# Graph layer and expert layer: node sums for two tiles at a time, gate logits by expert for four tiles at a time

## The chip, the core and the metric

The kernel runs on one core of one Trainium2 chip. A core has five engines with queues of their own: TensorE (PE, matrix products; its weight loads are shown apart as PEld), VectorE (DVE), ScalarE (ACT), GpSimd (POOL) and SyncE (SP), and 16 DMA engines that move data for all of them. PE writes into PSUM, from which DVE or ACT copy into SBUF. The metric is the time of one execution on the device in microseconds (us), as a median over several; every engine works through its own queue in order, and waits at semaphores for others.

## The reference, cut to what matters

There are N = 12500 nodes with D = 256 features, 212500 weighted edges sorted by destination (17 to a node on average), and E = 8 experts.

```
xn  = layernorm(x)
agg = segment_sum(xn[src] * edge_weight, dst)      # (N, 256)
x1  = x + agg @ W.T + b
t   = layernorm(x1)
logits = t @ gate_w + gate_b                       # (N, 8)
e   = argmax(softmax(logits));  p = its probability
# the first C = 1954 tokens of each expert are kept, in token order
y   = relu(t @ w1[e] + b1[e]) @ w2[e] + b2[e]      # hidden size 1024
out = x1 + nan_to_num(y * p * kept)
```

## The kernel before

A tile is 128 rows. Nodes make 98 tiles (the last has 84 rows), edges 1661 tiles.

**Start.** `table()` normalises x into the DRAM table `feat`, while the first 112 edge tiles are gathered from x itself.

**Main loop.** Each turn of the `while` loop near the end (L822) writes, in this order, one `gather` (L582, an indirect DMA on POOL's queue that fetches 128 source rows into a buffer `m`, of which there are 32), then at most one scatter from `pool_q` (or a step of a finished page's ending), some selection matrices `h` (`onehot`, L590), one `product` (L599: h.T @ m, added in PSUM over a group of 15 edge tiles; 16 turns behind its gather), one step of `nodes()` and one step of `experts()`. The generators' `yield`s set which turn an instruction is written in, and that order is kept on each engine's queue (the schedule is manual). Each group's sum is copied to an SBUF tile `ws` (L602) and stands in `sums`.

**Nodes.** Node rows and groups of edges don't line up. For a tile t, `groups_of(t)` gives the two or three groups that can hold its edges; `shift` (L608) makes for each a 128 x 128 matrix `s` of 0 and 1 (L612) that moves group rows to node rows, and L635 adds `sums[g].T @ s` for the two halves of the features. ACT copies the result (`aT`, L639), L644 multiplies by the weights, and DVE adds x and the bias into `rt` (L647, L648) and takes the statistics (L180, L181). A tile waits for its last group (`while gs[-1] not in sums`).

**Routing.** Tiles are taken in 14 chunks: eleven of eight tiles, then five, four and one. At a chunk's end `route` (L246) takes the root of the variance on ACT (L185) and inverts it on DVE, stores `rt` to `out`, and for each tile normalises (L214), transposes twice on PE (L271), copies to SBUF (`xT`, L274), multiplies with `gw_sb` (L279: the tokens are the weights, eight columns move through) and adds the bias (L281). Then come argmax (L296 to L306), prefix sums over tokens (L314, L315), the exponential (L317), the place of each token in the pages of its expert (L338), and `put`, a scatter per tile on POOL (L341). `listing` finds pages that are full; `last` lists the part-filled ones.

**Experts.** `experts` takes the pages in order. A page holds 128 tokens of one expert (some are taken as pairs). SP loads the page (`pg`, L439) and 2 MB of weights (L446 to L452), DVE normalises it (`xg`, L459), PE transposes it (L468), multiplies (L483, L494), and `finish` does the rest up to a scatter into `out` (`send`, L525, on POOL). A page starts at the earliest twenty turns after its load; steps of a single page are 2.3 turns apart. All PSUM tiles of nodes and routing come from one pool of two buffers (`psum`, L242); transposes of routing and of pages share one buffer (`pT`).

After the loop stand branches (`rest`, and a second way of summing) that the inputs here don't enter.

Of the kernel before, what the change touches and what calls it, by code (L numbers as in the profile page):

```python
# [94 lines left out]
def gnn_moe_kernel(ctx: ExitStack, tc: tile.TileContext, x, src, dst, ew, wT, gb, gate_w, gate_b,  # L95
# [13 lines left out]
    cols = consts.tile([P, P], F32, name="cols")  # L109
    nc.gpsimd.iota(cols, pattern=[[1, P]], base=0, channel_multiplier=0,  # L110
                   allow_small_or_imprecise_dtypes=True)
    pcol = consts.tile([P, 1], F32, name="pcol")
# [42 lines left out]
    gateb_sb = consts.tile([P, E], F32, name="gateb_sb")  # L155
# [63 lines left out]
    class Ffn:  # L219
# [26 lines left out]
        def route(self, rt, ln, t0, nt, rows):  # L246
# [9 lines left out]
            def normal(j):  # L256
                xn[j] = p3.tile([P, D], F32, name="xn1", bufs=3)
                ln_apply(xn[j][:rows, :], rt[:rows, j, :D], ln, r, j, rows)
# [7 lines left out]
            for j in range(nt):  # L266
                if j + 2 < nt:
                    normal(j + 2)
                pt = self.ps_t.tile([P, 512], F32, name="pT")
                for k in range(2):  # L270
                    nc.tensor.transpose(pt[:, k * P:k * P + rows], xn[j][:rows, k * P:(k + 1) * P],  # L271
                                        ident[:rows, :rows])
                xT = p3.tile([P, 2, P], F32, name="xT", bufs=3)
                nc.scalar.copy(xT[:, :, :rows],  # L274
                               pt[:, :2 * P].rearrange("p (k r) -> p k r", k=2)[:, :, :rows])
                yield
                pl = self.psum("pl")[:, :E]
                for k in range(2):
                    nc.tensor.matmul(pl[:rows, :], xT[:, k, :rows], gw_sb[:, k, :],  # L279
                                     start=(k == 0), stop=(k == 1))  # L280
                nc.vector.tensor_add(lgs[:rows, j, :], pl[:rows, :], gateb_sb[:rows, :])  # L281
# [277 lines left out]
    with tc.tile_pool(name="edges", bufs=1) as edges:  # L559
# [8 lines left out]
        with tc.tile_pool(name="p2", bufs=32) as p2, tc.tile_pool(name="p2h", bufs=12) as p2h, \  # L568
# [36 lines left out]
            def nodes():  # L605
                xs, shifts = [], {}

                def shift(t):  # L608

                    for g in groups_of(t) if t < NT else ():  # L610
                        s = p2o.tile([P, P], F32, name="s", bufs=8)
                        nc.vector.tensor_scalar(s, cols, float(P * t), win[:, g:g + 1], op0=ALU.add,  # L612
                                                op1=ALU.is_equal)
                        shifts[t, g] = s

                for c, (t0, nt, rows) in enumerate(CHUNKS):
                    rt = p3.tile([P, CH, RW], F32, name="rt")
                    ln = ln_new(p3)
                    for t in range(t0, t0 + nt):
# [5 lines left out]
                        if t == 0:  # L625
                            shift(t)
# [363 lines left out]
```

## Time and profile before

| | |
|---|---|
| median of three runs | 2569.41 us (2568.65 to 2575.24) |
| the profiled execution | 2575.36 us, its span 2573.6 us |
| mean granted clock of TensorE | 0.867 |
| POOL: gathers from `feat` (L582) | 1549, 972 ns each |
| PE: products of edges (L599) | 3322 passes, 451 ns each |
| PE: sums of nodes (L635) | 1116 passes, 299 ns each |
| PE: gate logits (L279) | 392 passes, 272 ns each |
| DVE: selection matrices s (L612) | 279, 308 ns each |

A line of a group gives the source line, the engine, the operation, the tiles (out<-in), shapes and count, then the busy time and the mean of one, then the engine's idle time just before and what ended it. In the order of time, a row has the start, the length, the engine, the line and the tiles; "x6" means six instructions in a row, and brackets give the idle time before and who ended it. Matmuls overlap in the records, so their pitch (the time between starts) is shorter than their listed length; an f32 matmul shows as two passes. A turn is one pass of the main loop.

### The profile page before, as it was taken

How to read it: one execution, taken by the hardware profiler on the slowest of the kernel's cores; microseconds unless marked ns; L12 is line 12 of the kernel's file. 1: busy time of each engine (PE TensorE's matmuls, PEld its weight loads, DVE VectorE, ACT ScalarE, POOL GpSimd, SP SyncE). 2: the span in 40 equal slices, each digit the busy share in tenths (PEclk: the TensorE clock that was granted, in tenths of full speed). 3: DMA queues.
4: the chain of work that ended last, by engine and by line, in shares of the span. 5: the costliest groups of instructions: out<-in, count | busy, mean ns of one | idle time of the engine just before them, and what ended most of it. 6: DMA issues, size and time to landing. Idle time of an engine off the chain costs nothing. (4 is left out here: it accounts for less than half of the span.)

```text
span 2573.6 us, 30236 instructions
## 1 busy us (share of the span) xinstructions
PE 2046.4 (80%) x9082; PEld 1599.7 (62%) x9082; DVE 1177.0 (46%) x4287; ACT 504.9 (20%) x1315; POOL 1805.4 (70%) x1859
## 2 busy tenths in 40 slices
PE   2467788797799698698699699698698797698797
PEld 1345545575577477477487487477476574487686
DVE  6775433444344344354453444444443443454432
ACT  5750000111012012012012012012011110122232
POOL 7647777777777777777777777777777777777111
PEclk9678666799799799799799799799799797799898
DMA  8759434644654654654654654654654354497485
GB/s 282 252 172 368 127 109 124 193 145 122 211 166 123 219 157 122 209 165 121 204 170 122 201 175 122 204 170 123 194 177 121 110 186 122 138 309 247 153 273 176
DMA packets 264700, 455.60 MB, mean 177 GB/s; under 512 B 44799, under 2 KB 190406, under 8 KB 264520
## 3 DMA queue, kind: packets, MB, share of 16 engines
q0 software_dynamic: 88800, 240.41, 30.5%
q1 hardware_dynamic: 136210, 174.68, 21.1%
q10 hardware_dynamic: 39510, 38.41, 4.6%
q8 instruction: 77, 1.26, 0.2%
q14 instruction: 103, 0.84, 0.1%
HBM read 387.86 MB, written 67.83 MB: 177 GB/s over the span
## 5 line engine op out<-in xcount | busy, mean ns | idle before, releaser
L582 POOL DMA_INDIRECT m<-feat,src_i x1549 | 1506.2, 972 | 493.0 <-issue 222.1
L599 PE MATMUL pw<-m,h 128*128 128x256 f32 x3322 | 1114.9, 451 | 408.7 <-DMA m<-feat,src_i 297.8
L599 PEld LDWEIGHTS pw<-m,h 128*128 128x128 f32 x3322 | 654.0, 219 | 701.9 <-DMA m<-feat,src_i 406.2
L590 DVE TENSOR_SCALAR h<-cols,rel,w_sb 128x128 f32<-128x128 f32 x1549 | 467.0, 360 | 405.6 <-PE pw L599 397.3
L483 PE MATMUL ph<-gT,w_sb 128*128 128x256 f32 (+1 forms) x1856 | 362.7, 346 | 0.0
L494 PE MATMUL py<-w_sb,hT 128*128 128x256 f32 x1456 | 349.8, 385 | 0.0
L483 PEld LDWEIGHTS ph<-gT,w_sb 128*128 128x128 f32 x1856 | 308.7, 199 | 33.3
L494 PEld LDWEIGHTS py<-w_sb,hT 128*128 128x128 f32 x1456 | 274.6, 193 | 35.1
L487 ACT ACTIVATE hT<-ph,b_sb 128x256 f32<-128x256 f32 (+1 forms) x464 | 167.9, 426 | 419.4 <-PE ph L483 409.7
L525 POOL DMA_INDIRECT out<-z,tok x91 | 91.1, 1001 | 153.2 <-DVE tok L522 111.7
L635 PEld LDWEIGHTS ms<-s,ws 128*128 128x128 f32 x1116 | 177.1, 216 | 18.2 <-issue 3.7
L635 PE MATMUL ms<-s,ws 128*128 128x128 f32 x1116 | 176.3, 299 | 3.4 <-DVE s L612 3.3
L647 DVE TENSOR_TENSOR rt<-xt,ms 128x256 f32<-128x256 f32 x98 | 41.2, 420 | 287.8 <-PE ms L644 287.7
L602 ACT COPY ws<-pw 128x256 f32<-128x256 f32 x111 | 41.4, 373 | 631.6 <-PE pw L599 631.6
L582 POOL DMA_INDIRECT m<-in_x,src_i x112 | 108.1, 965 | 53.6 <-issue 20.1
L504 DVE TENSOR_TENSOR y<-py,b_sb 128x512 f32<-128x512 f32 (+1 forms) x58 | 33.4, 576 | 240.4 <-PE py L494 240.4
L341 POOL DMA_INDIRECT buf<-rt,to x98 | 98.9, 1009 | 54.0 <-issue 19.2
L459 DVE TENSOR_SCALAR xg<-pg 128x256 f32<-128x256 f32 x91 | 35.3, 418 | 174.1 <-DMA pg<-buf 174.1
L507 ACT ACTIVATE y<-y,pg 128x256 f32<-128x256 f32 x91 | 42.6, 502 | 340.4 <-DVE y L504 294.5
L644 PE MATMUL ms<-wT_sb,aT 128*128 128x256 f32 x392 | 107.4, 399 | 2.4 <-ACT aT L639 2.4
L639 ACT COPY aT<-ms 128x256 f32<-128x256 f32 x98 | 36.5, 373 | 275.6 <-PE ms L635 269.9
L644 PEld LDWEIGHTS ms<-wT_sb,aT 128*128 128x128 f32 x392 | 77.4, 199 | 15.8 <-ACT aT L639 4.4
(159 smaller groups left out, 1253.6 us busy)
## 6 DMA issues: line engine op xcount, KB each, us to landing
w_sb<-in_w SPq DMA_DIRECT2D x116, 1024.0 KB, 11.4
m<-feat,src_i POOLq DMA_INDIRECT x1549, 2.8
buf<-fill SPq DMA_DIRECT2D x13, 1300.0 KB, 18.4
xt<-in_x ACTq DMA_DIRECT2D x97, 128.0 KB, 2.4
xt<-in_x SPq DMA_DIRECT2D x12, 1024.0 KB, 8.1
feat<-xn ACTq DMA_DIRECT2D x12, 1024.0 KB, 9.7
out<-rt ACTq DMA_DIRECT2D x11, 1024.0 KB, 4.9
pg<-buf SPq DMA_DIRECT2D x33, 260.0 KB, 13.4
```

What stands on the lines that cost most here:

```text
L341: s = nc.gpsimd.indirect_dma_start(out=buf[:, :], out_offset=bass.IndirectOffsetOnAxis(ap=to[:, j, :], axis=0), in_=rt[:rows, j, :], in_of ...
L483: nc.tensor.matmul(ph[:, c:c + n], w1_sb[:, k, f * P:(f + 1) * P], xT[:, k * n:(k + 1) * n], start=(k == 0), stop=(k == 1))
L487: nc.scalar.activation(hT[:, f, :n], ph[:, c:c + n], AF.Relu, bias=b1_sb[:, f:f + 1])
L494: nc.tensor.matmul(py[:, a, :], hT[:, f, a * P:(a + 1) * P], w2_sb[:, f, :], start=(f == 0), stop=(f == F // P - 1))
L507: nc.scalar.activation(y[:, a, :], y[:, a, :], AF.Copy, scale=pg[:, a, D + 2:D + 3])
L525: s = nc.gpsimd.indirect_dma_start(out=out[:, :], out_offset=bass.IndirectOffsetOnAxis(ap=to[:, a, :], axis=0), in_=z[:, a, :], in_offset= ...
L582: nc.gpsimd.indirect_dma_start(out=m, out_offset=None, in_=x[:, :] if k < RAW else feat[:, :], in_offset=bass.IndirectOffsetOnAxis(ap=src_ ...
L590: nc.vector.tensor_scalar(h, cols, rel[:, k:k + 1], w_sb[:, k:k + 1] if w is None else w, op0=ALU.is_equal, op1=ALU.mult)
L599: nc.tensor.matmul(product.pw, hs.pop(k), ms.pop(k), start=(j == 0), stop=last)
L602: nc.scalar.copy(ws, product.pw)
L635: nc.tensor.matmul(pa[:, k * P:(k + 1) * P], sums[g][:, k * P:(k + 1) * P], shifts[t, g], start=(g == gs[0]), stop=(g == gs[-1]))
L644: nc.tensor.matmul(px[:rows, :], aT[:, k * P:k * P + rows], wT_sb[:, k, :], start=(k == 0), stop=(k == 1))
```

## The change

The selection matrices become 256 columns wide: `turns` lists pairs of tiles within a chunk (a single one where a chunk is odd), `groups` the union of their groups, and `shift` makes one wide matrix for each group of the turn, with six buffers instead of eight. The sums are made for both tiles at once (256 columns move through PE for each group and half of the features), one ACT copy takes them (512 columns, one buffer instead of two), and the projection follows tile by tile, with a step of its own for each. The loads of x keep two tiles ahead of a pair, with five buffers.

In `route`, transposes of two tiles fill one PSUM tile and one copy takes them to `xT`, which now holds four tiles in one buffer. Then `gw_sb` is the weights (eight columns) and up to 512 tokens move through; the logits come out with experts on partitions. ACT adds the bias from `gateb_sb`, now one value per partition, into `lT`; PE transposes each tile's part back (eight columns each), and one DVE copy fills `lgs` for four tiles.

```diff
@@ -106,9 +106,10 @@
     make_identity(nc, ident)
     ones = consts.tile([P, P], F32, name="ones")
     nc.vector.memset(ones, 1.0)
-    cols = consts.tile([P, P], F32, name="cols")
-    nc.gpsimd.iota(cols, pattern=[[1, P]], base=0, channel_multiplier=0,
+    cols2 = consts.tile([P, 2 * P], F32, name="cols")
+    nc.gpsimd.iota(cols2, pattern=[[1, 2 * P]], base=0, channel_multiplier=0,
                    allow_small_or_imprecise_dtypes=True)
+    cols = cols2[:, :P]
     pcol = consts.tile([P, 1], F32, name="pcol")
     nc.gpsimd.iota(pcol, pattern=[[1, 1]], base=0, channel_multiplier=1,
                    allow_small_or_imprecise_dtypes=True)
@@ -152,7 +153,7 @@
     gb_sb = consts.tile([P, D], F32, name="gb_sb")
     wT_sb = consts.tile([P, 2, D], F32, name="wT_sb")
     gw_sb = consts.tile([P, 2, E], F32, name="gw_sb")
-    gateb_sb = consts.tile([P, E], F32, name="gateb_sb")
+    gateb_sb = consts.tile([E, 1], F32, name="gateb_sb")
 
     keep = ctx.enter_context(tc.tile_pool(name="keep", bufs=1))
     run = keep.tile([P, E], F32, name="run")
@@ -254,7 +255,7 @@
             xn = {}
 
             def normal(j):
-                xn[j] = p3.tile([P, D], F32, name="xn1", bufs=3)
+                xn[j] = p3.tile([P, D], F32, name="xn1", bufs=4)
                 ln_apply(xn[j][:rows, :], rt[:rows, j, :D], ln, r, j, rows)
 
             for j in range(min(nt, 2)):
@@ -263,22 +264,38 @@
             nc.vector.tensor_copy(rt[:rows, :nt, D:D + 1], ln[1][:rows, :nt, 0:1])
             nc.vector.tensor_copy(rt[:rows, :nt, D + 1:D + 2], r[:rows, :nt, None])
             yield
-            for j in range(nt):
-                if j + 2 < nt:
-                    normal(j + 2)
-                pt = self.ps_t.tile([P, 512], F32, name="pT")
+
+            for j0 in range(0, nt, 4):
+                n4 = min(4, nt - j0)
+                xT = p3.tile([P, 2, 4 * P], F32, name="xT", bufs=1)
+                for j1 in range(j0, j0 + n4, 2):
+                    n2 = min(2, nt - j1)
+                    pt = self.ps_t.tile([P, 512], F32, name="pT")
+                    for j in range(j1, j1 + n2):
+                        if j + 2 < nt:
+                            normal(j + 2)
+                        for k in range(2):
+                            c = (k * n2 + j - j1) * P
+                            nc.tensor.transpose(pt[:, c:c + rows], xn[j][:rows, k * P:(k + 1) * P],
+                                                ident[:rows, :rows])
+                    c = (j1 - j0) * P
+                    n = (n2 - 1) * P + rows
+                    nc.scalar.copy(xT[:, :, c:c + n], pt[:, :2 * n2 * P].rearrange(
+                        "p (k r) -> p k r", k=2)[:, :, :n])
+                    yield
+                    yield
+                n = (n4 - 1) * P + rows
+                pl = self.psum("pl")
                 for k in range(2):
-                    nc.tensor.transpose(pt[:, k * P:k * P + rows], xn[j][:rows, k * P:(k + 1) * P],
-                                        ident[:rows, :rows])
-                xT = p3.tile([P, 2, P], F32, name="xT", bufs=3)
-                nc.scalar.copy(xT[:, :, :rows],
-                               pt[:, :2 * P].rearrange("p (k r) -> p k r", k=2)[:, :, :rows])
+                    nc.tensor.matmul(pl[:E, :n], gw_sb[:, k, :], xT[:, k, :n], start=(k == 0),
+                                     stop=(k == 1))
+                lT = p3.tile([E, 4 * P], F32, name="lT", bufs=1)
+                nc.scalar.activation(lT[:, :n], pl[:E, :n], AF.Identity, bias=gateb_sb)
                 yield
-                pl = self.psum("pl")[:, :E]
-                for k in range(2):
-                    nc.tensor.matmul(pl[:rows, :], xT[:, k, :rows], gw_sb[:, k, :],
-                                     start=(k == 0), stop=(k == 1))
-                nc.vector.tensor_add(lgs[:rows, j, :], pl[:rows, :], gateb_sb[:rows, :])
+                pb = self.psum("pb")[:, :4 * E].rearrange("p (j e) -> p j e", e=E)
+                for j in range(n4):
+                    nc.tensor.transpose(pb[:rows, j, :], lT[:, j * P:j * P + rows], ident[:E, :E])
+                nc.vector.tensor_copy(lgs[:rows, j0:j0 + n4, :], pb[:rows, :n4, :])
             yield
 
             def small(name, last=E, dt=F32):
@@ -605,48 +622,64 @@
             def nodes():
                 xs, shifts = [], {}
 
-                def shift(t):
-
-                    for g in groups_of(t) if t < NT else ():
-                        s = p2o.tile([P, P], F32, name="s", bufs=8)
-                        nc.vector.tensor_scalar(s, cols, float(P * t), win[:, g:g + 1], op0=ALU.add,
-                                                op1=ALU.is_equal)
-                        shifts[t, g] = s
-
+
+                turns = [(t, min(2, t0 + nt - t)) for t0, nt, _ in CHUNKS for t in range(t0, t0 + nt, 2)]
+
+                def groups(i):
+                    t, n = turns[i]
+                    return range(groups_of(t)[0], groups_of(t + n - 1)[-1] + 1)
+
+                def shift(i):
+
+                    for g in groups(i) if i < len(turns) else ():
+                        t, n = turns[i]
+                        s = p2o.tile([P, 2 * P], F32, name="s", bufs=6)
+                        nc.vector.tensor_scalar(s[:, :n * P], cols2[:, :n * P], float(P * t),
+                                                win[:, g:g + 1], op0=ALU.add, op1=ALU.is_equal)
+                        shifts[i, g] = s
+
+                turn = 0
                 for c, (t0, nt, rows) in enumerate(CHUNKS):
                     rt = p3.tile([P, CH, RW], F32, name="rt")
                     ln = ln_new(p3)
-                    for t in range(t0, t0 + nt):
-                        for i in range(len(xs), min(t + 3, NT)):
-                            x_ = p3.tile([P, D], F32, name="xt", bufs=4)
+                    while turn < len(turns) and turns[turn][0] < t0 + nt:
+                        t1, n = turns[turn]
+                        for i in range(len(xs), min(t1 + n + 2, NT)):
+                            x_ = p3.tile([P, D], F32, name="xt", bufs=5)
                             r = min(P, N - i * P)
                             nc.scalar.dma_start(x_[:r, :], x[i * P:i * P + r, :])
                             xs.append(x_)
-                        if t == 0:
-                            shift(t)
-                        gs = groups_of(t)
+                        if turn == 0:
+                            shift(0)
+                        gs = groups(turn)
                         while gs[-1] not in sums:
                             yield
                         yield
-                        pa = ffn.psum("pa")[:, :2 * P]
-                        aT = p2o.tile([P, 2 * P], F32, name="aT")
+                        pa = ffn.psum("pa")
+                        aT = p2o.tile([P, 2, 2 * P], F32, name="aT", bufs=1)
                         for k in range(2):
                             for g in gs:
-                                nc.tensor.matmul(pa[:, k * P:(k + 1) * P],
-                                                 sums[g][:, k * P:(k + 1) * P], shifts[t, g],
+                                nc.tensor.matmul(pa[:, k * n * P:(k + 1) * n * P],
+                                                 sums[g][:, k * P:(k + 1) * P],
+                                                 shifts[turn, g][:, :n * P],
                                                  start=(g == gs[0]), stop=(g == gs[-1]))
                             yield
-                        nc.scalar.copy(aT, pa)
-                        shift(t + 1)
+                        nc.scalar.copy(aT[:, :, :n * P],
+                                       pa[:, :2 * n * P].rearrange("p (k r) -> p k r", k=2))
+                        turn += 1
+                        shift(turn)
                         yield
-                        px = ffn.psum("px")[:, :D]
-                        for k in range(2):
-                            nc.tensor.matmul(px[:rows, :], aT[:, k * P:k * P + rows], wT_sb[:, k, :],
-                                             start=(k == 0), stop=(k == 1))
-                        x1 = rt[:rows, t - t0, :D]
-                        nc.vector.tensor_add(x1, xs[t][:rows, :], px[:rows, :])
-                        nc.vector.tensor_add(x1, x1, gb_sb[:rows, :])
-                        ln_stats(ln, x1, t - t0, rows)
+                        for t in range(t1, t1 + n):
+                            px = ffn.psum("px")[:, :D]
+                            a = (t - t1) * P
+                            for k in range(2):
+                                nc.tensor.matmul(px[:rows, :], aT[:, k, a:a + rows], wT_sb[:, k, :],
+                                                 start=(k == 0), stop=(k == 1))
+                            x1 = rt[:rows, t - t0, :D]
+                            nc.vector.tensor_add(x1, xs[t][:rows, :], px[:rows, :])
+                            nc.vector.tensor_add(x1, x1, gb_sb[:rows, :])
+                            ln_stats(ln, x1, t - t0, rows)
+                            yield
                     yield from ffn.route(rt, ln, t0, nt, rows)
                     pool_q.extend(ffn.put)
                     last = c == len(CHUNKS) - 1
@@ -810,7 +843,7 @@
                             product(k)
                 nc.sync.dma_start(gb_sb, gb.partition_broadcast(P))
                 nc.sync.dma_start(gw_sb, gate_w.rearrange("(k p) e -> p k e", p=P))
-                nc.sync.dma_start(gateb_sb, gate_b.partition_broadcast(P))
+                nc.sync.dma_start(gateb_sb, gate_b.rearrange("(e a) -> e a", a=1))
                 return n * RB
 
             done = table()
```

## The prediction

> **What bounds the kernel now.** I read the page's first two parts, then POOL in the order of time, then PE in the order of time from the last gather on, then PE and the clock by stretches.
>
> The busiest engine by share is PE (80%), POOL has 70%. The order of time says otherwise:
>
> ```profile
> PE 2046.4 (80%) x9082; PEld 1599.7 (62%) x9082; DVE 1177.0 (46%) x4287; ACT 504.9 (20%) x1315; POOL 1805.4 (70%) x1859
> ...
> POOL 7647777777777777777777777777777777777111
> ```
>
> ```profile
> 931.35 0.95 POOL L582 DMA_INDIRECT m<-feat,src_i  x1 [0.30 <-PE ph L483]
> 932.60 0.94 POOL L582 DMA_INDIRECT m<-feat,src_i  x1 [0.30 <-PE pw L599]
> ...
> 2378.56 0.95 POOL L582 DMA_INDIRECT m<-feat,src_i  x1 [0.30 <-issue]
> 2379.82 1.00 POOL L525 DMA_INDIRECT out<-z,tok  x1 [0.30 <-issue]
> 2388.39 1.00 POOL L525 DMA_INDIRECT out<-z,tok  x1 [7.57 <-DVE tok L522]
> ```
>
> Each gather of 128 rows takes 0.95 us and 0.30 us follows it; from 190 us to the last gather at 2378.56 no gap of POOL is longer than 0.31, whatever the releaser named. About 1710 indirect DMAs stand there, 1.28 us each: 2190 us. So three stages: a start to 182 us, a body at POOL's pace, and a tail of 181 us from the last gather to the last instruction at 2559.8 (14 us of ending follow in the span).
>
> In the body PE waits for gathers, 297.8 us in the list of waits. From a product's end to the issue of the gather that takes its buffer again I find at least 29 us, and from a chunk's destinations (L338) to its first scatter at least 7.6 us. PE work in the body is covered by these.
>
> The tail is PE's (its last matmul ends there), with idle time:
>
> ```profile
> 2384.50 0.59 PE L599 MATMUL pw<-m,h 128*128 128x256 f32 x2
> 2384.93 1.78 PE L635 MATMUL ms<-s,ws 128*128 128x128 f32 x12
> 2387.18 1.13 PE L644 MATMUL ms<-wT_sb,aT 128*128 128x256 f32 x4 [0.46 <-ACT aT L639]
> 2388.15 3.73 PE L483 MATMUL ph<-gT,w_sb 128*128 128x128 f32 x32
> 2394.76 0.41 PE L468 MATMUL pT<-ident,xg 128*128 128x128 f32 x2 [2.88 <-DVE xg L459]
> ...
> 2415.41 0.41 PE L468 MATMUL pT<-ident,xg 128*128 128x128 f32 x2 [3.34 <-DVE xg L459]
> ...
> 2434.18 0.41 PE L468 MATMUL pT<-ident,xg 128*128 128x128 f32 x2 [2.82 <-DVE rt L264]
> ...
> 2445.51 0.20 PE L424 MATMUL ms<-c,page_of 128*1 128x8 f32 x2 [6.05 <-DVE c L422]
> ...
> 2453.34 0.44 PE L468 MATMUL pT<-ident,xg 128*128 128x128 f32 x2 [0.99 <-DVE xg L459]
> ```
>
> ```profile
> 2392.40:2395.80 3.40, 1.03 (x6) 0.99 (x7) 2.36 (x11) 1.83 (x7) 0.00 (x0) 0.99 1.08 373
> 2395.80:2402.60 6.80, 6.34 (x20) 4.91 (x19) 0.49 (x2) 0.74 (x2) 0.00 (x0) 0.50 0.06 16
> ...
> 2457.10:2558.60 101.50, 96.40 (x649) 88.75 (x647) 38.67 (x124) 40.00 (x130) 12.66 (x13) 1.00 0.84 268
> ```
>
> (Columns: stretch, length, busy us of PE, PEld, DVE, ACT, POOL, granted clock, DMA share, GB/s.) After a stretch with little PE work the clock is 0.50 for the next. From 2457.1 on the clock is 1.00 and expert pages follow each other at 7.58 us. Between 2384.9 and 2457.1 the last nodes are routed: 72.2 us, for four pages (about 30 us) and some 11 us of node work.
>
> **The change part by part.** Pitches at full clock: a 128-column pass 0.111 us (six from 912.47 to 913.14), a 256-column pass 0.216 (eight L494 in 1.73). An f32 matmul is two passes.
>
> *Work on PE.* Sums: 1116 passes of 128 columns, 124 us, become 764 of 256 and 20 of 128 (196 pairings of group and turn, not 279; two halves, two passes): 167 us, +43. Logits: 392 passes at 0.09 (four in 0.36), 35 us; after, 24 groups x 4 passes of 512 columns at 0.43, 41 us, and 98 small transposes at about 0.11, 11 us: +17. Together +60 us of PE, nearly all in the body, under the waits for gathers: 0. Without that cover it would be +60.
>
> *DVE and ACT.* Selection tiles: 279 x 0.236 = 66 us become 196 wide ones at 0.29 to 0.41 (L513 and L459, 256 columns), 57 to 80. Logit evictions: 98 x 0.166 become 26 x 0.2, -11. ACT: 196 copies x 0.372 = 73 become 100 x 0.5 and 26 logit evictions of 0.5, -10. In the body these are slack: 0. What they can still do is slow POOL. The Trainium skill ("GPSIMD Engine Reference", Specifications) has GpSimd's SBUF interfaces shared with VectorE, contended by its two-port modes; this speaks against wider one-source instructions, and the added 14 us at most, charged in full, would be +14. The row: the gather at 932.60 ran beside three selection tiles (932.19 to 932.86) in 0.94, the fastest there is. I take 0, range -2 to +4.
>
> *Order.* The written order of the changed kernel has every later step of a chunk, and every expert page, exactly four turns of the main loop later relative to the gathers; the scatters' and sends' order on POOL is the same, but one send moves behind the last gather: -1.3 us. Loads on SP move with their pages and stay behind the same scatters. The x loads on ACT's queue are issued in pairs, one more buffer deep: 0.
>
> *The tail*, walked along PE's new order. (a) Last product. Before it ends 6.4 us after its gather's issue, since PE still had 17 us of work in its last 14 turns (17.9 us of POOL). The new order has there 14 products (6.0) and one page (7.2), 13.2 us, so PE waits for the gather; a product can end 3.5 us after it. I take -2.2, with the send 2384.9 becomes 2381.4. (b) To the first page's transposes: the half page moved behind (0.2 + 1.7 + 1.7), the pair's sums (16 passes, 3.5 against 1.3; four groups against three), two projections (1.7 against 0.9), first layer 3.5: 12.3 us. DVE is late: after the first projection (at 8.2) two tiles of 1.6 each, the page's ending 2.0, variance, root 0.2 or with its table 1.5, inverse 1.0, two normalised tiles 0.7: 15.7 to 17.0. Queued behind it: the transposes of the first pair, ACT's copy, then the page's own (one PSUM buffer): 17.0 to 18.3. Station at 2399 against 2394.8. (c) To the second page's transposes: 2.0 + 2.0 for the page and the second pair, logits 1.7, wait for their eviction 0.9, small transposes and DVE's argmax unhidden 2.0, prefix 0.3, first layer 3.6, wait 0.9, list 0.6: 14.0 us, against 20.7, of which 3.3 are the wait for xg. (d) To the third: sums and projection of the last tile as before, the wait for L394 now under half a page: 12.2 against 18.8. (e) To the fourth: the wait of 6.05 now has the first layer in its middle: 11.8 against 19.2. (f) 3.7 as before; then the same 13 pages.
>
> At full clock the new walk is 17.6 + 14.0 + 12.2 + 11.8 + 3.7 = 59.3. The old one by the same pitches is 9.0 + 17.3 + 14.2 + 16.1 + 3.7 = 60.3, and took 72.2: 12 us went to the half clock. So (b) to (f) turn on the clock. The Trainium skill ("TensorE: Matmul & The Clock Gate", What's actually happening) lets the clock fall after at least one idle window of about 3.4 us; by that only the gap of 6.05 would cost, some 3 us, and the new order, with no gap above about 4, would lose nothing. The row above shows a stretch of 3.4 us with 1.03 busy followed by 0.50, so gaps under 3 us suffice. The old order has four such falls (27 us at 0.50); the new one keeps the gap at (b), now 3.4, and the thin logits, and loses two shorter ones: I take 8 us lost instead of 12, between 3 and 15.
>
> Sum: -1.3 - 2.2 - 1.0 - 4.0 = -8.5; small waits that I can't see at each new hand-over (lT, pb, two-tile copies: about 0.2 to 0.5 each, three to a chunk, two chunks) give back 2.5: **-6 us**. The profiled execution took 2575.4 (span 2573.6 and 1.8 around it) against the median 2569.4; I subtract from the median: **2563.4 us**.
>
> **The rivals.**
> *It cancels.* The last product isn't earlier and the clock falls as before: -1.3 - 1.0 + 2.5 = 0: 2569.5. For it: the four gaps have the same causes. Against: 13.2 us of work in 17.9.
> *The clock stays up.* Only 3 us are lost: -13: 2556. Against: gap (b) alone costs some 3.
> *Slower: the last pair.* Before, tile 95 was summed under the gathers; now it waits for group 110 with tile 96. (b) then costs 18.3 - 9.8 = +8.5 with the late root. If its gap and the thin logits behind it hold the clock at 0.50 through (c) (+5), and a full PE leaves (a) at -1.3, and half of (d) and (e) is lost, it is +8: 2577. It decides when (c) takes as long as before, 20 us.
> *PE becomes the bound* of the body by +60 us of columns: 29 us of slack in buffers and 298 of waits speak against; 2580 and more if it were. It is in the slower case.
> *It doesn't do what it says*: fewer instructions but more PE time is in fact so in the body; it just doesn't reach the end.
>
> **How the numbers follow.** Likeliest (tail shorter, 2557 to 2569): 0.45. Cancels: 0.27. Clock stays up: 0.13. Slower: 0.15. About 0.3%, 7.7 us, is what a measurement can tell from no change: faster means below 2561.7, slower above 2577.1. Faster: a third of the likeliest, all of the clock case and a little of the cancelling: 0.31. Slower: most of its case: 0.13. Same: 0.56. The range, with POOL's contention and both ends of the clock: 2553 to 2577.
>
> **What would show it.** POOL's body still has gaps of 0.30 only, and the last gather falls 0 to 4 us earlier; the last product ends some 4 us after its gather's issue; the first page's transposes in the tail come near 2399 with a gap of 3 to 4 before the transposes of xn; no gap of 6 before the matmul of last(); clean pages (7.58 us) begin 3 to 12 us earlier. Wrong if POOL gaps above 0.3 appear in the body, if gathers lengthen beside wide selection tiles, or if half-clock stretches in the tail exceed 27 us.

## The result

The changed kernel takes 2579.04 us in the median of nine runs (2576.06 to 2583.68), the kernel before 2569.41 us (2565.22 to 2576.07): ratio 1.0034, interval 1.0021 to 1.0047. It is slower by 0.34%, about 10 us, where 2563.4 was forecast, and lies just outside the range.

The profiled execution took 2582.74 us, span 2580.9. First the page's shares and its POOL row, then POOL in the order of time:

```profile
PE 2064.3 (80%) x8560; PEld 1558.2 (60%) x8560; DVE 1180.6 (46%) x4132; ACT 504.8 (20%) x1245; POOL 1811.3 (70%) x1859
...
POOL 7647777777777777777777777777777777777111
```

```profile
956.46 0.95 POOL L599 DMA_INDIRECT m<-feat,src_i  x1 [0.30 <-PE pw L616]
957.71 2.15 POOL L599 DMA_INDIRECT m<-feat,src_i  x1 [0.30 <-issue]
960.16 0.95 POOL L599 DMA_INDIRECT m<-feat,src_i  x1 [0.30 <-PE ms L676]
...
2383.73 0.97 POOL L599 DMA_INDIRECT m<-feat,src_i  x1 [0.30 <-issue]
2385.00 1.00 POOL L542 DMA_INDIRECT out<-z,tok  x1 [0.30 <-DVE s L637]
2392.05 1.00 POOL L542 DMA_INDIRECT out<-z,tok  x1 [6.05 <-issue]
```

The body is still POOL's, with gaps of 0.30 us (one of 0.49, at 2364.3). But the last gather starts at 2383.73, 5.2 us later than before, though one indirect DMA (1.28 us) has left the body: its 1708 indirect DMAs take 979.2 ns on the mean, against 975.4, which is 6.5 us. The gaps have not grown (from 200 us to the last gather they add up to 519.1 us, before 519.7); single gathers have. One of them is the row of 957.71: 2.15 us instead of 0.95. VectorE's rows over the same stretch, in the order of time:

```profile
956.57 1.11 DVE L607 TENSOR_SCALAR h<-cols,rel,w_sb 128x128 f32<-128x128 f32 x4
957.59 1.14 DVE L637 TENSOR_SCALAR s<-cols,win 128x256 f32<-128x256 f32 x4
958.65 0.42 DVE L528 TENSOR_SCALAR fin<-y 128x512 uint8<-128x512 f32 x1
958.98 0.42 DVE L530 TENSOR_SCALAR hi<-y 128x512 f32<-128x512 f32 x1
959.32 0.42 DVE L533 TENSOR_SCALAR z<-y 128x512 f32<-128x512 f32 x1
959.93 0.42 DVE L679 TENSOR_TENSOR rt<-xt,ms 128x256 f32<-128x256 f32 x1 [0.19 <-PE ms L676]
```

The gather starts 0.12 us into a row of four wide selections, and ends at 959.86, 0.12 us after `z`, the last VectorE instruction of an unbroken stretch. The group of selections in the two lists of groups, of before and of after:

```profile
L612 DVE TENSOR_SCALAR s<-cols,win 128x128 f32<-128x128 f32 x279 | 65.8, 308 | 0.0
```

```profile
L637 DVE TENSOR_SCALAR s<-cols,win 128x256 f32<-128x256 f32 (+1 forms) x196 | 64.7, 368 | 124.6 <-PE ms L662 122.7
```

VectorE is busy with them no longer than before, 64.7 us for 65.8. The pitch inside a row of them went from 0.196 to 0.263 us, and a new idle time stands before them: with six buffers VectorE waits for PE to read an old `s`. The prediction had not seen that wait.

The tail, PE in the order of time:

```profile
2385.95 0.60 PE L616 MATMUL pw<-m,h 128*128 128x256 f32 x2
2388.86 0.70 PE L616 MATMUL pw<-m,h 128*128 128x256 f32 x2 [2.31 <-DMA m<-feat,src_i]
2389.40 3.27 PE L500 MATMUL ph<-gT,w_sb 128*128 128x128 f32 x16
2392.46 1.39 PE L616 MATMUL pw<-m,h 128*128 128x256 f32 x4
...
2408.75 0.76 PE L279 MATMUL pT<-ident,xn 128*128 128x128 f32 x4 [2.47 <-DVE xn L215]
2410.19 0.66 PE L485 MATMUL pT<-ident,xg 128*128 128x128 f32 x2 [0.68 <-ACT xT L283]
...
2441.61 0.66 PE L485 MATMUL pT<-ident,xg 128*128 128x128 f32 x2 [2.81 <-DVE rt L265]
...
2454.43 0.19 PE L441 MATMUL ms<-c,page_of 128*1 128x8 f32 x2 [1.81 <-DVE c L439]
```

and by stretches (columns as in the prediction: stretch, length, busy us of PE, PEld, DVE, ACT and POOL, granted clock, DMA share, GB/s):

```profile
2386.40:2389.80 3.40, 1.09 (x7) 0.89 (x7) 0.00 (x0) 0.94 (x4) 0.00 (x0) 1.00 1.03 371
2389.80:2393.20 3.40, 3.40 (x16) 3.31 (x16) 0.00 (x0) 0.49 (x2) 1.00 (x1) 0.50 0.73 248
2464.20:2565.70 101.50, 96.43 (x649) 88.77 (x647) 38.66 (x124) 39.89 (x130) 12.63 (x13) 1.00 0.83 268
```

The last product ends at 2393.85, 10.1 us after its gather's issue (before: 6.5). From there to the clean pages (2464.2) it is 70.3 us, against 72.0; the pages are the same, 7.58 us each. So between the two profiles: +5.2 to the last gather, +3.6 to the last product, -1.7 in the walk behind it, together +7.1; PE's last matmul ends 7.1 us later, the execution took 7.4 us more. The medians lie 9.6 apart. One profile is one execution: a second one of the kernel before took 2565.05 us, 10.3 less than the first, and 6.7 of that are shorter gathers (971.5 ns on the mean). Single profiles show where time sits, the medians what a thing costs.

In three batches of the runs below (e5 to e8, e13 to e16, e17 and e18; called the batches of 3.5 ms) every kernel, the one before too, took 3.4 to 3.6 ms, with POOL busy for half of the span, so that their times can't tell 0.3% on a body at POOL's pace; of them single indirect DMAs are read.

### The profile page after: what moved, and what is told of

Same layout as the page of the kernel before. It is cut to its first block, busy times and chain, and to the rows that moved or that the text cites. A ratio compares the mean times of both kernels' runs of the same rounds, so it can differ in the third digit from the quotient of the medians.

```text
span 2580.9 us, 28796 instructions
## 1 busy us (share of the span) xinstructions
PE 2064.3 (80%) x8560; PEld 1558.2 (60%) x8560; DVE 1180.6 (46%) x4132; ACT 504.8 (20%) x1245; POOL 1811.3 (70%) x1859
## 5 line engine op out<-in xcount | busy, mean ns | idle before, releaser
L616 PE MATMUL pw<-m,h 128*128 128x256 f32 x3322 | 1085.7, 450 | 403.8 <-DMA m<-feat,src_i 296.3
L616 PEld LDWEIGHTS pw<-m,h 128*128 128x128 f32 x3322 | 666.2, 218 | 724.2 <-DMA m<-feat,src_i 394.0
L607 DVE TENSOR_SCALAR h<-cols,rel,w_sb 128x128 f32<-128x128 f32 x1549 | 478.1, 364 | 467.5 <-PE pw L616 455.9
L500 PE MATMUL ph<-gT,w_sb 128*128 128x256 f32 (+1 forms) x1856 | 356.0, 342 | 0.0
L662 PE MATMUL ms<-s,ws 128*128 128x256 f32 (+1 forms) x784 | 200.9, 403 | 0.1
L662 PEld LDWEIGHTS ms<-s,ws 128*128 128x128 f32 x784 | 161.5, 208 | 26.4 <-DVE rt L679 0.2
L637 DVE TENSOR_SCALAR s<-cols,win 128x256 f32<-128x256 f32 (+1 forms) x196 | 64.7, 368 | 124.6 <-PE ms L662 122.7
L488 ACT COPY gT<-pT 128x512 f32<-128x512 f32 (+1 forms) x58 | 28.8, 497 | 287.6 <-PE pT L485 267.3
```

Of the source, the lines that this page charges most:

```text
L500: nc.tensor.matmul(ph[:, c:c + n], w1_sb[:, k, f * P:(f + 1) * P], xT[:, k * n:(k + 1) * n], start=(k == 0), stop=(k == 1))
L607: nc.vector.tensor_scalar(h, cols, rel[:, k:k + 1], w_sb[:, k:k + 1] if w is None else w, op0=ALU.is_equal, op1=ALU.mult)
L616: nc.tensor.matmul(product.pw, hs.pop(k), ms.pop(k), start=(j == 0), stop=last)
L637: nc.vector.tensor_scalar(s[:, :n * P], cols2[:, :n * P], float(P * t), win[:, g:g + 1], op0=ALU.add, op1=ALU.is_equal)
L662: nc.tensor.matmul(pa[:, k * n * P:(k + 1) * n * P], sums[g][:, k * P:(k + 1) * P], shifts[turn, g][:, :n * P], start=(g == gs[0]), stop=( ...
```

## The experiments

Three explanations stood against each other. **Contention**: wide selections hold up the gathers, where VectorE and GpSimd share something. **VectorE's wait**: the new wait for `s` buffers bunches VectorE's work, or delays the matrices `h`. **Order and tail**: everything four turns later, a later last product.

All kernels compute the whole result.

**Each half of the change alone (e1, e2).** e1 has the new `nodes` with the old `route`, e2 the new `route` with the old `nodes`.

> The changed node sums (pairs of tiles, wide selection matrices) with the old route. Theory 1, bursts: a gather on POOL whose start falls into a run of wide selection matrices on VectorE is held until the run ends, so the gathers' mean rises from 975 to about 979 ns and the last gather comes 4 to 7 us later than before; time 2574 to 2580 us. Theory 2, order: it is the later place of all steps against the gathers that lengthens them (here two turns later, not four); then about half of it, 2571 to 2575 us. Theory 3, routing: the new logits cost it; then 2566 to 2571 us here.

> The changed logits (experts as columns, four tiles at a time) with the old sums of one tile and narrow selection matrices. Theory 1, bursts: no wide selection matrices, the gathers' mean stays within 2 ns of 975, the last gather within 2 us of 2378.6; time 2565 to 2572 us. Theory 2, order: about half of the loss, 2571 to 2575 us. Theory 3, routing: the whole loss, 2576 to 2581 us.

e1: 2582.76 us beside 2572.36 of before on the same chip, ratio 1.0035 (1.0022 to 1.0048). e2: 2570.56, 0.9989 (0.9980 to 0.9998). The whole loss is in the sums of two tiles; the gate logits by expert are a small gain, if any: it lies under the 0.3% that can be told, and its repeat (e16) fell into a batch of 3.5 ms, where 1.0002 (0.9982 to 1.0023) says nothing of it.

**VectorE's stretches spread out (e3).** `shift` only notes the selections of the next pair; `one_shift` writes one of them per turn while the pair waits for its last group, and the rest behind the wait.

```
         while gs[-1] not in sums:
+            one_shift()
             yield
+        one_shift(True)
         yield
```

> The changed kernel, with its wide selection matrices written one per turn of the main loop while the node generator waits for its last group, instead of all of a pair's three to five in one go; the same instructions, the same number of turns. Theory 1, bursts: gathers over 1.4 us beside selection matrices go, the gathers' mean falls back to about 975 ns, the last gather comes 4 to 7 us earlier than in the changed kernel; time 2571 to 2576 us. If it is the amount of wide selection work and not its being back to back, nothing changes: 2577 to 2581 us. Theory 2, order: nothing changes.

2578.75 us, 1.0029 (1.0022 to 1.0037). VectorE's wait for PE is gone (its idle time before `s` is 0.0 instead of 124.6), and the loss remains:

```profile
L643 DVE TENSOR_SCALAR s<-cols,win 128x256 f32<-128x256 f32 (+1 forms) x196 | 62.2, 354 | 0.0
```

The 2571 to 2576 us forecast from contention in long rows missed. The edit spread less than was meant, as 15 rows of four selections still ran back to back, so it does not test that forecast fully.

**Order alone (e4).** The kernel before, with four empty turns at the start of `route`.

```
             p3 = self.p3
+            for _ in range(4):
+                yield
             yield
```

> The kernel before, with four empty turns at the start of each chunk's route, so that all later steps of the chunk and the expert pages stand four turns later against the gathers, as they do in the changed kernel. Theory 1, bursts: the body doesn't change, the last gather within 2 us of 2378.6; the tail may move by up to 5 us either way: 2566 to 2574 us. Theory 2, order: the gathers lengthen as in the changed kernel and the last product comes about 10 us after its gather's issue: 2575 to 2581 us.

2574.12 us, 1.0004 (0.9994 to 1.0014): no measurable cost, at most 3.6 us. Its last product ends 9.0 us after the gather's issue, nearly as late as in the changed kernel; POOL's row, then PE's:

```profile
2376.54 1.17 POOL L584 DMA_INDIRECT m<-feat,src_i  x1 [0.30 <-issue]
```

```profile
2384.80 0.69 PE L601 MATMUL pw<-m,h 128*128 128x256 f32 x2 [0.41 <-DMA m<-feat,src_i]
```

So the later last product alone doesn't explain the loss.

**The width alone (e5, again as e9).** The kernel before with its 279 selections made 256 columns wide; the matmuls still read 128 of them. The tiles `s` and `cols` double with them; no other instruction moves.

```
-    s = p2o.tile([P, P], F32, name="s", bufs=8)
-    nc.vector.tensor_scalar(s, cols, float(P * t), win[:, g:g + 1], op0=ALU.add,
+    s = p2o.tile([P, 2 * P], F32, name="s", bufs=8)
+    nc.vector.tensor_scalar(s, cols2, float(P * t), win[:, g:g + 1], op0=ALU.add,
...
-    sums[g][:, k * P:(k + 1) * P], shifts[t, g],
+    sums[g][:, k * P:(k + 1) * P], shifts[t, g][:, :P],
```

> The kernel before, with each of its 279 selection matrices made 256 columns wide, of which the sums read the first 128 as before; nothing else changes. Theory A, two-port work: wide selection work on VectorE holds up the gathers on POOL by its amount; the changed kernel shows some 0.04 us for each wide matrix, the old one 0.015, so 279 x 0.025 = +7 us in the body: 2576 to 2583 us on a chip where before takes 2572. Theory B, order and tail: the widths don't matter, it is the pairs' place in the turns and behind the last gather: 2570 to 2574 us.

> The kernel before with its 279 selection matrices 256 columns wide, once more, on a chip where before takes about 2570 us (on the last chip everything took 3.4 to 3.5 ms and time told nothing, but the gathers' mean rose from 966.7 to 972.6 ns). Theory A, two-port work of wide matrices: ratio to before 1.002 to 1.004, the last gather 5 to 10 us later. Theory B, order and tail: ratio 0.999 to 1.001.

e5: 3494.67 us, 0.9972, in a batch of 3.5 ms (e8, the kernel before there, 3488.35 in its one run). e9: 2579.94 beside 2570.76, ratio **1.0034 (1.0021 to 1.0048)**: 9.2 us. That this equals the loss of the whole change is chance in part, since e9 widens 279 selections and the changed kernel makes 196. Its order is that of before, and its last product ends 7.3 us after the gather's issue (6.5 and 7.2 in the two profiles of before). The group in its profile:

```profile
L613 DVE TENSOR_SCALAR s<-cols,win 128x256 f32<-128x256 f32 x279 | 87.1, 365 | 0.0
```

21.3 us more of VectorE work, on an engine that is busy for 46% of the span. In its profile the body's gathers take 977.0 ns on the mean, against 975.4 and 971.5 in those of before. The run of the kernel before in that batch (e12) is the second profile named above. Its last gather starts at 2370.91, where every explanation had it within 4 us of 2378.6: two profiles of one kernel lie as far apart there as the change and the kernel before.

**Narrow instructions in the changed kernel (e6, again as e10).** The tile `s` stays 256 wide and is written by two instructions of 128.

```
-    nc.vector.tensor_scalar(s[:, :n * P], cols2[:, :n * P], float(P * t),
-                            win[:, g:g + 1], op0=ALU.add, op1=ALU.is_equal)
+    for a in range(n):
+        nc.vector.tensor_scalar(s[:, a * P:(a + 1) * P], cols, float(P * (t + a)),
+                                win[:, g:g + 1], op0=ALU.add, op1=ALU.is_equal)
```

> The changed kernel, each wide selection matrix written by two instructions of 128 columns (387 narrow ones in place of 196 wide). Theory A, if a gather waits as long as the back-to-back run lasts: runs grow from 1.05 us (four at 0.263) to 1.57 (eight at 0.196), so 3 to 6 us more than the changed kernel: 2582 to 2588 us where before takes 2572. If only wide instructions hold the port and narrow ones let gathers in between: 4 to 6 us less than the changed kernel, 2574 to 2578 us. Theory B: as the changed kernel within 2 us, 2579 to 2583 us.

> The changed kernel with each wide selection matrix written by two narrow instructions, once more (on the last chip its gathers' mean was 965.8 ns against 966.7 of before). Theory A in the form that narrow instructions let gathers in between: the body's loss goes, the last gather within 2 us of before's, and what is left over before is the tail's: ratio 0.999 to 1.0015. Theory B: as the changed kernel, 1.0025 to 1.004.

e6: 3482.44 us, 0.9940, in the same batch as e5. e10: 2575.28 us beside 2570.76, 1.0015 (1.0007 to 1.0023). VectorE works longer on them:

```profile
L638 DVE TENSOR_SCALAR s<-cols,win 128x128 f32<-128x128 f32 x387 | 87.2, 306 | 112.2 <-PE ms L663 112.2
```

87.2 us for 64.7, and yet the loss is 4.5 us instead of 9.6, so that about half comes back. So VectorE's busy time isn't what costs; the form of the instruction matters.

**More buffers (e7, again as e11).** Ten tiles `s` instead of six (and 28 buffers `m` instead of 32 to make room).

> The changed kernel with ten buffers for wide selection matrices instead of six (and, for the room, 28 instead of 32 for gathered rows). With six, VectorE waits 123 us in all for PE to read the pair's matrices before it can write the next pair's, and then catches up in one run. Theory C, this wait makes the runs that hold up the gathers: the wait goes to under 10 us, gathers over 1.4 us fall to the 13 of before, time 2572 to 2576 us where before takes 2572. Theory A: the wait goes, the gathers stay as they are: 2578 to 2583 us.

> The changed kernel with ten buffers for wide selection matrices and 28 for gathered rows, once more. Theory C, the wait of VectorE for a free matrix makes the runs: ratio 0.999 to 1.0015 to before. Theory A: the wait goes and the loss stays: 1.0025 to 1.004.

e7: 3372.34 us against 3504.09, in the same batch as e5; why it is 3.8% under the kernel before there wasn't followed. e11: 2579.08 us, 1.0032 (1.0021 to 1.0043). The wait is gone and the loss is not; VectorE's wait costs nothing that shows:

```profile
L637 DVE TENSOR_SCALAR s<-cols,win 128x256 f32<-128x256 f32 (+1 forms) x196 | 59.4, 364 | 0.0
```

**What the gathers show.** An undisturbed gather takes 0.94 us in every trace (the fifth percentile, 942 to 945 ns). For the body's indirect DMAs, from one profile each:

```
                       selections    mean, ns          beyond 0.945 in those   longer than
                                                       over 1.345 us, us       1.4 us
before, two profiles   279 narrow    975.4 971.5       11.0  8.5               13  10
e2, e4 (old nodes)     279 narrow    973.6 975.2       10.2 12.0               12  15
e9 (old nodes)         279 wide      977.0             18.6                    25
after                  196 wide      979.2             20.0                    24
e1, e3, e11            196 wide      977.7 977.3 977.9 15.0 16.1 16.7          19  21  21
e10                    387 narrow    977.9             12.3                    15
```

The kernels with wide selections and the first four don't overlap in any column. Their means lie 3.9 ns apart (977.8 and 973.9), over 1708 indirect DMAs 6.7 us; the long gathers differ by as much, 6.9 us (17.3 and 10.4). e10 is with the narrow ones in long gathers, and with the wide ones in the mean. Why, shows when the time is split by what ran on VectorE meanwhile. Each indirect DMA from 200 us to the last gather counts with what it takes beyond 0.942 us, as "beside `s`" if a selection runs during it, and otherwise as "other":

```
                                     beside s, us           other, us
before (two), e2, e4   279 narrow    7.5  5.6  5.4  6.8     46.4 41.6 44.9 46.9
e9                     279 wide      13.6                   42.1
after, e1, e11         196 wide      11.1 11.1 9.8          50.1 47.5 49.1
e3 (spread out)        196 wide      18.3                   39.5
e10                    387 narrow    6.9                    51.4
```

In e9 the wide selections take 7.3 us more than the narrow ones of the first row, of the 9.2 us that it lost, and nothing is added elsewhere. In the changed kernel (third row) it is 4.3 us beside selections, and 4.0 us beside other work or none. e10 has the first part back and keeps the second, which fits the half of the loss that it keeps. In e3 the selections stand beside more gathers and the split shifts; its sum of 57.8 is near the others'. So, by these profiles, width explains about half of the changed kernel's loss. What lengthens the other gathers in the new sums is not shown.

The long ones say it more sharply. Apart from one at the start of the body, which overlaps VectorE's instructions of 1.89 us on the tile `good` and comes in nearly every kernel, the indirect DMAs over 1.4 us beside two or more selections are: with narrow ones none in before (twice), e2, e6, e8 and e16, and two each in e4 and e10; with wide ones 12 in e9, 7 to 9 in the changed kernel, e1, e3 and e11, and 9 and 8 in e5 and e7.

Seven of the changed kernel's eight stand in rows of four. Nearly every pair touches four groups, but only 19 times do the four selections run back to back; otherwise VectorE waits for a buffer between them. Where a gather starts 0.07 to 0.12 us after the row's first, it takes 1.84 us (four times) or over 2.1 (twice, with `fin`, `hi`, `z` behind), and 0.27 us after it 1.41 (once). But 0.18 us after it (once) it takes 0.98, and 0.08 us before it (twice) 0.94; there the row takes 0.1 us more.

**Where the operand is read (e13 and e14, e15, with e16 beside them; again e17, e18).** The column numbers that are compared come from PSUM; width, number and order of the selections stay. A bank is freed by letting the sums of even and odd groups share one.

```
+    pw2 = ps_e.tile([P, 2 * D], F32, name="pw")
+    cols_p = ps_c.tile([P, 256], F32, name="cols_p")
+    nc.vector.tensor_copy(cols_p, cols2)
...
-    product.pw = ps_e.tile([P, D], F32, name="pw")
+    product.pw = pw2[:, k // G % 2 * D:(k // G % 2 + 1) * D]
...
-    nc.vector.tensor_scalar(s[:, :n * P], cols2[:, :n * P], float(P * t),
+    nc.vector.tensor_scalar(s[:, :n * P], cols_p[:, :n * P], float(P * t),
```

> The changed kernel, whole computation, with the column numbers that the wide selections s are compared with read from PSUM instead of SBUF (the two halves of one bank now hold the sums of even and odd groups, so that a bank is free for them); the 196 wide selections stay and each may take longer on VectorE. Theory A (the wide selections hold up the gathers at the SBUF ports that VectorE and GpSimd share, and an operand in PSUM frees them): 2566 to 2573 us, and no run of four s stretches a gather past 1.4 us. Theory B (the gathers suffer from how long VectorE is busy at a stretch, or the loss is in the order of the work): 2576 us or more, since s gets no shorter.

> As the run before, and the 1661 matrices h read their columns from PSUM too. Theory A: most of the 60 us that gathers take over their undisturbed 942 ns goes, some 20 to 40 us of it, so 2535 to 2555 us. Theory B: 2576 us or more.

> The kernel before with the new route alone, s (one tile wide) and h with columns in PSUM. Theory A: 2530 to 2550 us, faster than both kernels; if it is level with the run before, two tiles at a time cost nothing once the ports are free. Theory B: 2566 to 2575 us, as the new route alone.

> The kernel before with the new route alone, once more on the chip of these runs: 2564 to 2571 us under both theories, 0.1% under the kernel before; it is what the run with s from PSUM is to be held against.

> The changed kernel with the columns of the wide selections s in PSUM, once more, since every kernel of the first batch took 3.5 ms and its times tell nothing on a difference of 0.3%. Theory A (the ports): 2566 to 2573 us, although each s takes some 0.1 us longer from PSUM (473 against 368 ns in the first batch). Theory B (VectorE's stretches, or the order): 2578 us or more.

> The kernel before with the new route alone, s and h with columns in PSUM, once more for the same reason. In the first batch its gathers took 960.4 ns on the mean against 965.5 ns with the columns in SBUF. Theory A: 2550 to 2565 us. Theory B: 2566 to 2575 us.

All in batches of 3.5 ms: e13 3525.85 us (1.0067), e14 3533.41 (1.0090), e15 3527.16 (1.0064), e16 3503.64 (1.0002), e17 3566.97 (1.0060), e18 3550.97 (1.0009). None is faster than before there, and the forecasts in microseconds stay untested. The traces have matched pairs, though. In the ten-buffer kernel (e7, columns in SBUF) a send starts 0.38 us after the first of four `h`, with four wide `s` right behind them; VectorE's rows, then POOL's:

```profile
1015.23 1.11 DVE L607 TENSOR_SCALAR h<-cols,rel,w_sb 128x128 f32<-128x128 f32 x4
1016.26 1.14 DVE L637 TENSOR_SCALAR s<-cols,win 128x256 f32<-128x256 f32 x4
1017.31 0.41 DVE L679 TENSOR_TENSOR rt<-xt,ms 128x256 f32<-128x256 f32 x1
```

```profile
1015.61 1.91 POOL L542 DMA_INDIRECT out<-z,tok  x1 [5.81 <-DVE h L607]
```

In e13 (columns of `s` in PSUM) a send starts in the same phase, 0.37 us after the first of the four `h`:

```profile
1907.81 1.11 DVE L611 TENSOR_SCALAR h<-cols,rel,w_sb 128x128 f32<-128x128 f32 x4
1908.84 1.65 DVE L641 TENSOR_SCALAR s<-cols_p,win 128x256 f32<-128x256 f32 x4
```

```profile
1908.18 1.10 POOL L542 DMA_INDIRECT out<-z,tok  x1 [14.11 <-DVE tok L539]
```

1.91 us became 1.10, though the selections behind it last longer (a pitch of 0.392 for 0.263). This phase comes three times in e7 (1.91 each) and five times in e13 and e17 (1.10 each). Behind the first such row, at the start of the body, no indirect DMA beside one of the 35 rows of four `s` in e13 and e17 took more than 1.10 us (17 rows had one beside them); beside the 46 in e7 (36 had one) eight took 1.53 to 2.03. And by the count above, over 1.4 us beside two or more selections, e13, e14 and e17 have none, for the 8 of e7. VectorE does the same work for longer, and the indirect DMA passes: the place it reads from decides. That is contention at SBUF, shown on single indirect DMAs; that the time would follow at the usual pace is not shown.

e14's part missed: with `h` in PSUM too, the mean of the body's indirect DMAs stayed (962.6 ns for e13's 962.4), where 20 to 40 us were forecast to go. With `s` one tile wide and `h`, both from PSUM, it is 960.4 ns in e15 and 963.4 in e18, against 965.5 in e16.

At the usual pace no kernel clearly beats the one before; the nearest is e2, the route alone, at 0.9989.

## Why the prediction was wrong, step by step

**The pace.** Right: POOL's body sets the time, and a tail of PE follows. "No gap longer than 0.31" overlooked one of 0.44 us at 1273.8; the one of 0.49 us after is as harmless, since the gaps' sum stayed.

**PE's columns, taken as 0.** Right in what it cost, by PE's waits for gathers, before and after:

```profile
PE pw L599 <- DMA m<-feat,src_i: 297.8, 343, 3.3
```

```profile
PE pw L616 <- DMA m<-feat,src_i: 296.3, 311, 4.6
```

The size was off, +60 us of passes against 17.9 more busy time on the page, where overlapping passes count once.

**POOL's contention, taken as 0 between -2 and +4.** This is the step that failed, and the sign that the prediction had named for it came: gathers lengthen beside wide selections. Between the two profiles the body's indirect DMAs take 6.5 us more. Widening all 279 selections costs 9.2 us (e9), which for the change's 196 would be 6.5 by their number (an estimate); the split of the traces has 4.3 beside selections and about as much beside other work, which the step had not in it at all. The forecast named a charge of up to +14 by the Trainium skill ("GPSIMD Engine Reference", Specifications: SBUF interfaces shared with VectorE), weighed a row against it and followed the row. The row was true and didn't bear on the case. Its gather began at 932.60, 0.41 us into the three narrow selections and 0.26 before their end, in one phase; the change made wide ones, of which the trace of before had none. The profile of before held better rows: its 13 gathers over 1.4 us were there to be read and were not, such as this one beside `fin`, `hi` and `z` of 512 columns:

```profile
1034.94 2.48 POOL L582 DMA_INDIRECT m<-feat,src_i  x1 [0.30 <-issue]
```

The Trainium skill comes nearer in "SBUF — State Buffer" (SBUF: two separate sides): a DMA issued from GpSimd's queue can't write its descriptors while VectorE runs an instruction that takes both ports. The trace agrees in kind. In size it shows more than one instruction's length: the gather of 957.71 stood through seven instructions in a row. That an operand in PSUM rules out the two-port mode is stated in "VectorE: DVE Perf Modes" (Why PSUM operands drop a tier) of the Trainium skill, and agrees with the pitches, 0.392 us from PSUM and 0.263 from SBUF for the same 256 columns.

**DVE's slack, taken as 0.** Right for its own time, though the wait of 124.6 us for buffers of `s` was overlooked; e3 and e11, where it is gone, lose as much as the change.

**Order: four turns later, one send behind the last gather, -1.3.** Right: e4 measures no cost, and one more send stands behind the last gather (25 indirect DMAs there for 24).

**Tail (a), -2.2.** Wrong too: +3.6, an error of 5.8 us beside contention's 6.5. PE does run out of work and wait for the last gathers, as written. But the clock of the next 3.4 us was not in the step: 1.09 busy in 3.40 us, then 0.50, with half a page's first layer in front of the last products. The data was later too: in the stretch of that wait the DMA engines are full (share 1.03, 371 GB/s) with a page's weights, issued at 2381.67 and 2382.29. e4 has nearly as late a product without a measurable loss, so this alone did not make the change slower; it is part of why the sum lies so far above the forecast.

**Tail (b) to (f), -2.5.** Right in the sum, -1.7, but by luck, since its parts are off. The five stations took 16.3, 18.3, 13.1, 18.5 and 4.1 us, for 17.6, 14.0, 12.2, 11.8 and 3.7 at full clock and 10.5 of half clock and small waits not laid to any; (e), which was to gain the most, gained 0.7. The first transposes of the last pair came 14.9 us after the last product, with a gap of 2.47 before them (3 to 4 forecast), and the wait of 6.05 us fell to 1.81. The stretches at half clock add to 23.9 us for 27.3. Where the prediction let a row decide against a rule of the Trainium skill on the clock ("TensorE: Matmul & The Clock Gate", What's actually happening), the rows after repeat that row: a stretch of 3.4 us with 1.09 us of PE work is followed by 0.50.

**The rivals.** "Slower: the last pair" had the sign and nearly the size, 2577, by another mechanism, so by luck: its place, the tail behind the last product, was 1.7 us faster. Between the two profiles the loss is 6.5 us of longer gathers, -1.3 for the send, +3.6 and -1.7: +7.1, where -6 was forecast. Contention stood in the range as a bound, and the bound was too narrow.

What stays open: what lengthens the gathers beside other work in the new sums, the half of the loss that narrow instructions (e10) don't bring back; whether the operand in PSUM gives time back at the usual pace; and how far the 0.1% of the route alone is real.

## What to carry to other kernels

Where a body runs at the pace of indirect DMAs on GpSimd's queue, VectorE's slack isn't free: look for gathers longer than the undisturbed one and for what VectorE does beneath them, before taking a wider one-source instruction from SBUF as hidden. A row settles a question only if it has the form, width and phase of what the change adds; else keep the bound of the rule in the range. Test such a cost by doing the widening alone in the old kernel: one run separated it from order, buffers and tail. Then count how much of it the changed kernel has; an equal total is not an equal cause.

## What the hardware showed beyond expectation

A gather can be held for a whole unbroken row of VectorE instructions, not for one: 2.15 us at 957.71 for 0.94 undisturbed, released 0.12 us after the last of seven. Its phase decides: begun 0.08 us before the row, the gather takes 0.94, begun 0.1 us after the row's start 1.84, and begun 0.18 us after it 0.98. Width and length of the row both count. Behind 200 us, the indirect DMAs beside a row take beyond 0.942 us each: 0.08 and 0.05 us a row beside three narrow selections in the two profiles of before (82 rows each), 0.15 beside three wide ones in e9 (82 rows), 0.43 beside four wide ones in the changed kernel (18 rows) and 0.21 in e11 (46 rows), 0.26 beside eight narrow ones in e10 (18 rows).

Executions of one kernel differ in part by their gathers: the two profiles of before, 10.3 us apart, have 6.7 us of it there.
